# Denominators and first values of self-attention in one run of narrow products

## The chip, the core and the metric

The kernel runs on one core of one Trainium2 chip. A core has several engines that work at the same time, each with its own queue, which it works off in order: TensorE (PE in the profile, with its weight loads as PEld), VectorE (DVE), ScalarE (ACT), GpSimd (POOL), and SyncE (SP), which here mostly issues DMA transfers. They meet through semaphores. The metric is the device time of one execution in microseconds (us); less is better. The median of three runs stands for a kernel.

## The reference

A decoder layer (causal self-attention, cross-attention to 64 context rows, feed-forward), and then a gated fusion with the context. Only the self-attention matters here; batch 4, 1024 rows, 512 features, 16 heads of 32:

```python
B, T, TE, C, H = (2, 1024, 1024, 512, 16)   # the inputs have batch 4
DH = C // H
q = jnp.einsum('btc,hcd->bhtd', xn, Wq) + bq[None, :, None, :]
...
scale = DH ** (-0.5)
scores = jnp.einsum('bhtd,bhsd->bhts', q, k) / scale
...
scores = jnp.where(mask[None, None], scores, -jnp.inf)
attn = jax.nn.softmax(scores, axis=-1)
out = jnp.einsum('bhts,bhsd->bhtd', attn, v)
```

The kernel doesn't divide each weight by its row's sum. It sums `exp(score - max) * v` and, apart from that, `exp(score - max)` alone. The second is the denominator; cross-attention's first steps divide by it.

## The kernel before

Three phases follow each other: self-attention, cross-attention, feed-forward. Self-attention goes on until about 960 us of the profile, with cross-attention's first steps beginning shortly before that.

**Units.** Self-attention is cut into 32 units, one for each batch, group of four heads (4 x 32 = 128 partitions) and half of the eight row tiles: four tiles of 128 query rows, 512 columns (`TG`). For one pair of units per head group these are tiles (0, 1, 6, 7) and (2, 3, 4, 5); in the first pair (0..3) and (4..7). A unit goes over the blocks of 128 keys that its tiles can see: eight blocks or six. A later block is seen by fewer tiles, so it has fewer columns: 512, 384, 256 or 128. The blocks are taken in a written-out order, in the eight-block unit for instance 0, 7, 2, 1, 3, 6, 4, 5.

**One block.** `exps` makes transposed scores for each of the four heads (`st`, PE, line 677), their exponentials (ACT, line 682) into a pair of tiles `pT` with two heads each, and, where the block lies on the diagonal of one of the unit's tiles, zeroes what is masked (POOL, line 690). `weigh_all` makes the weighted values of two blocks at a time, one block after its exponentials: for each block four products with 32 columns of values as weights, one for each head (`av`, line 707), which add up in one bank over all blocks. Then `weigh` adds the block's `pT` pair to the pair of the unit's first block (POOL, now and then DVE, line 729), so that the first block's tiles end as the sum over all blocks. They are overwritten in place, so the first of these additions waits until the first block's own values are made.

**Denominators.** `sums` multiplies the finished pair with a matrix of ones, 128 x 32, again four products for the four heads (`den`, line 740), copies them out of PSUM (ACT, line 743) and stores them with one or two DMAs (SP, line 746). PSUM for `den` is one of the three banks that `st` uses. The values have one bank, copied out at the end of a unit (line 732).

The products `av` and `den` are fp32 with 128 x 32 weights: each is two records in the profile, and the four heads' products stand in four different groups of 32 columns. All other products of the phase have weights of 128 columns. They are called wide in this text, and `av` and `den` narrow.

**Beside it.** While a unit's blocks are worked, PE also makes the row maxima of later units (`s`, line 622, reduced by DVE) and projects queries, keys and values of later units (`pq`, `pk`, `pv`, line 116). `run` (line 129) merges such lists of steps by the share of each that is left. The resulting program is then reordered by a scheduler, which places each engine's instructions by priority and by its own idea of when they are ready. `tc.high_priority` raises the priority of what is written inside it; `tc.issue_after(x)` keeps instructions of x's engine behind x. In `weigh_all` the first product of a pair of blocks is written plainly, and the others are held behind it with a raised priority.

**Where the denominators are placed.** `attend` returns its steps and, apart from them, `sums` as a step of its own. The loop over the units puts the `sums` of one unit behind the first 12 steps of the next one's (`den_at` is 0, `HG` 4), and the last unit's after the loop.

Of the kernel before, what the change touches and what calls it, by code (L numbers as in the profile page):

```python
# [9 lines left out]
F32 = mybir.dt.float32  # L10
# [7 lines left out]
P = 128  # L18
B, T, C, H = 4, 1024, 512, 16
DH = C // H  # L20
# [4 lines left out]
TG = 512  # L25
NJ = TG // P
NG = T // TG
NT = T // P
HG = P // DH
# [22 lines left out]
def decoder_then_fusion(ctx: ExitStack, tc: tile.TileContext, x, ctxT, cols, rows,  # L52
                        Wq_s, Wk_s, Wv_s, W1, Wq_c, Wk_c, Wv_c, W2, Wf1, Wf2,
                        Wt, WvT, WgT, out):
    nc = tc.nc
# [73 lines left out]
    def run(*streams, speed=None, sooner=None):  # L129


        speed = [v for v, s in zip(speed or [1.0] * len(streams), streams) if s]
        sooner = [v for v, s in zip(sooner or [0] * len(streams), streams) if s]
        streams = [s for s in streams if s]
        left = [sum(t for t, _ in s) or 1 for s in streams]
        total, at = list(left), [0] * len(streams)
        while any(i < len(s) for i, s in zip(at, streams)):
            k = min((k for k in range(len(streams)) if at[k] < len(streams[k])),
                    key=lambda k: (1 - left[k] / total[k]) / speed[k])
            t, f = streams[k][at[k]]  # L140
# [65 lines left out]
    den_dram = dram_tiles("dend", groups, [H, TG])  # L206
# [180 lines left out]
    def self_attention(ph):  # L387
# [8 lines left out]
        outp = ph.enter_context(tc.tile_pool(name="out_a", reuse_waits="tile", bufs=2))  # L396
# [19 lines left out]
        def psum(name):  # L416
# [9 lines left out]
                                fill=MASKED, base=0, pattern=[[-1, P]], channel_multiplier=1)  # L426
# [4 lines left out]
        ones = cst.tile([P, DH], F32, tag="ones", name="ones")  # L431
# [14 lines left out]
        AHEAD = 4  # L446
# [120 lines left out]
        units = [(b, g, h, tiles) for b in range(B) for g in range(NC) for h, tiles in enumerate(tiles_of(b, g))]  # L567
        order = list(range(KST))
# [86 lines left out]
                nc.scalar.dma_start(raw(qs[KS + k : KS + k + 1].rearrange("p r (j q) -> p (r j) q", q=P)),  # L655
                                    raw(mT[k]))

        def attend(u):

            b, g, h, tiles = units[u]  # L660

            order = Z["o%d" % tiles[-1]] if tiles[0] != 4 else Z["o9"]
            first_col = [P * sum(tile < kb for tile in tiles) for kb in range(tiles[-1] + 1)]
            last = order[-1]
            held = {}
# [29 lines left out]
            def weigh_all(kbs):  # L695

                if kbs[0] == order[0]:
                    held["av"] = ps_av.tile([P, TG], F32, tag="av", name=f"av_{u}")
                    todo = [(kb, r) for kb in kbs for r in range(HG)[::-1]]
                else:  # L700
                    todo = [(kb, r) for kb in kbs[::-1] for r in range(HG)[::-1]]
                if kbs[-1] == last:
                    todo = [(kb, r) for kb in sorted(kbs, key=lambda k: k == last) for r in range(HG)[::-1]]

                def one(kb, r):
                    c0 = first_col[kb]
                    return nc.tensor.matmul(held["av"][r * DH : (r + 1) * DH, c0:],  # L707
                                            v_at[b, g][:, kb, r * DH : (r + 1) * DH],
                                            held[kb][r // 2][:, r % 2, c0:], start=kb == order[0], stop=kb == last)
                if Z["hp"]:  # L710
                    lead = todo[0]
                    first = one(*lead).ins
                    with tc.issue_after(first), tc.high_priority(offset=Z["hp"]):
                        for at in todo[1:]:
                            one(*at)
                else:
                    for at in todo:
                        one(*at)
                for kb in kbs:
                    weigh(kb)  # L720

# [13 lines left out]
                            nc.sync.dma_start(av_dram[b, n, g][:, shared[1]], avs[:, shared[0]])  # L735

            def sums():
                den = ps_of[Z["den"]][0].tile([P, TG], F32, tag=ps_of[Z["den"]][1], name=f"den_{u}")
                for r in range(HG)[::-1]:
                    nc.tensor.matmul(den[r * DH : (r + 1) * DH, :], ones, held[0][r // 2][:, r % 2, :],  # L740
                                     start=True, stop=True)
                dens = outp.tile([P, TG], F32, tag="dens", name=f"dens_{u}", bufs=1)
                nc.scalar.copy(dens, den)
                for n in range(NG):
                    if shared := columns(tiles, n):
                        nc.sync.dma_start(den_dram[b, n][g * HG : (g + 1) * HG, shared[1]], dens[::DH, shared[0]])

            groups_of = [order[i : i + Z["grp"]] for i in range(Z["grp0"], len(order), Z["grp"])]
            if Z["grp0"]:
# [3 lines left out]
            steps = []  # L753
            for i in range(len(order) + Z["lag"]):
# [75 lines left out]

        pieces[Z["pf"]].append((0, prefetch))
        begun = []
        before, first_late = [], len(units) - AHEAD
        for u in range(len(units)):
            if u and u + 2 < len(units):
                load_stacks(u + 2, u)
            main, after = attend(u)
            n = u % 2
            ahead, begun = begun, []
            if not ahead and u + 1 < len(units):  # L840
                ahead = maxima(u + 1)
            if u and u + 2 < len(units) and Z["phi%d" % n]:
                begun = maxima(u + 2)
                k = Z["phi%d" % n]
                first = begun[: k]
                first.insert(Z["tpl"], ahead.pop())
                ahead, begun = ahead + first, begun[k:]
            if u == first_late:
                fronts_of.close()
                rest = late_steps()  # L850
                total = sum(t for t, _ in rest)
            if u >= first_late:
                fill, part = [], Z["late"][u - first_late] * total
# [5 lines left out]
            run(main[: 3 * HG + Z["den_at"]] + before + main[3 * HG + Z["den_at"] :], ahead, fill, speed=(Z["main"], (Z["ahead%d" % n] if u < Z["alf"] else Z["ahead_l"]) if u else Z["a0"], Z["fill"]), sooner=(Z["so0"], Z["so1"], Z["so2"]))  # L859
            before = after  # L860
        run(before)
        switch(None)()


# [648 lines left out]
```

## Time and profile before

| What | us |
|---|---|
| Runs | 2229.69, 2229.91, 2230.17 |
| Median | 2229.91 |
| The profiled execution | 2232.46 |
| Its span, first to last instruction | 2230.7 |
| Granted clock of TensorE, mean | 0.976 |
| 256 records of `den`, first to last start | 118.8 to 955.2 |
| Copies of `den`, 32, median of one | 0.585 |
| Stores of `den`, 62, median of one issue on SP | 0.494 |
| 369 additions (line 729) on POOL, busy | 543.4 |
| 256 masks (line 690) on POOL, busy | 107.0 |

The page divides the span into 40 slices of 55.8 us. Each digit is a busy share in tenths:

```profile
PE   6899999999999998959999998999999999999997
...
POOL 3178778777977887865555423010115103410414
PEclk9899999999999999979999999999999999999998
```

The first seventeen slices are self-attention.

In the profile's timelines each row is a stretch of equal instructions: start, duration of the whole row, engine, line, operation, what is written and read, and xN for N records. A row's idle time and what ended it stand in square brackets, where there was any. Matmuls overlap: one begins before the last one has ended, so the distance between starts says more than the durations do. In the rows of waits the numbers are the sum in us, the count, and the longest.

### The profile page before, as it was taken

The page shows a single profiled execution, that of the slowest core. Times are in us where ns is not written, and L with a number is a line of the kernel's source. Part 1 is how long each engine was busy: PE and PEld are TensorE (multiplying, and loading weights), DVE is VectorE, ACT ScalarE, POOL GpSimd, SP SyncE. Part 2 cuts the span into 40 slices and gives each one's busy share as a digit, 9 for nine tenths or more (in the row PEclk, how much of TensorE's full clock was granted, in tenths as well). Part 3 has the DMA queues.
Part 4 walks back from the last instruction along what each step waited for, and adds up shares of the span by engine and source line. Part 5 has one row for each costly group of instructions (what it writes and reads, how often), then busy time and mean ns, then how long its engine had stood idle before and what let it go on. Part 6 is the DMA issues. An engine that isn't in the chain of part 4 may idle for free.

```text
span 2230.7 us, 34011 instructions
## 1 busy us (share of the span) xinstructions
PE 2121.8 (95%) x11724; PEld 1607.5 (72%) x11724; DVE 1293.2 (58%) x2829; ACT 982.3 (44%) x2171; POOL 1091.8 (49%) x1156
## 2 busy tenths in 40 slices
PE   6899999999999998959999998999999999999997
PEld 5666676667666655548788886888887887888785
DVE  6476657665656678687878765341337225531727
ACT  3355455545555555435555565432233324322432
POOL 3178778777977887865555423010115103410414
PEclk9899999999999999979999999999999999999998
DMA  8855666655656475432222214644345425342531
GB/s 247 239 166 163 179 175 179 171 172 169 190 149 188 127 210 177 155 97 67 86 76 76 91 48 156 195 164 142 127 140 206 166 98 207 138 175 85 207 133 47
DMA packets 204386, 333.68 MB, mean 150 GB/s; under 512 B 28460, under 2 KB 91676, under 8 KB 202934
## 3 DMA queue, kind: packets, MB, share of 16 engines
q1 hardware_dynamic: 186364, 314.68, 45.1%
q10 hardware_dynamic: 17850, 16.83, 2.5%
q8 instruction: 93, 1.52, 0.3%
q14 instruction: 79, 0.65, 0.1%
HBM read 231.78 MB, written 99.12 MB: 148 GB/s over the span
## 4 chain that ended last, share of the span: by engine, by line
PE 77%; DVE 9%; DMA 5%; issue 5%; ACT 2%; POOL 1%; SPq 1%; DVEq 0%; POOLq 0%; ACTq 0%
PE ph_f L116 13%; PE acc_f L1251 13%; PE st L677 6%; PE s L622 6%; PE av L707 5%; PE pk L116 4%; PE po_c L116 4%; PE pv L116 4%; PE pq L116 4%; PE pq_x L116 3%; PE po_x L116 3%; PE pg_o L116 3%; PE sc_c L104 2%; PE av_c L1030 2%; PE tpp_c L1017 1%
## 5 line engine op out<-in xcount | busy, mean ns | idle before, releaser
L729 POOL TENSOR_TENSOR pT<-pT,pT 128x512 f32<-128x512 f32 (+3 forms) x369 | 543.4, 1495 | 34.8 <-PE av L707 29.3
L1251 PE MATMUL acc_f<-wf,hs_f 128*128 128x512 f32 x1536 | 385.6, 394 | 9.1 <-DVE hs_f L74 5.9
L116 PE MATMUL ph_f<-xn_f,wf 128*128 128x512 f32 x1536 | 382.5, 394 | 4.0 <-DVE xn_f L74 3.3
L682 ACT ACTIVATE pT<-st 128x512 f32<-128x512 f32 (+2 forms) x640 | 319.9, 560 | 128.4 <-PE st L677 87.4
L1251 PEld LDWEIGHTS acc_f<-wf,hs_f 128*128 128x128 f32 x1536 | 285.2, 188 | 72.6 <-DVE hs_f L74 8.1
L116 PEld LDWEIGHTS ph_f<-xn_f,wf 128*128 128x128 f32 x1536 | 288.5, 189 | 66.0 <-DVE xn_f L74 3.7
L627 DVE CUSTOM_DVE_ANT_0 s<-s,mask 128x512 f32<-128x512 f32 (+3 forms) x512 | 245.4, 503 | 142.1 <-PE s L622 140.9
L622 PE MATMUL s<-ks,qs 96*128 96x512 f32 (+3 forms) x768 | 253.4, 373 | 23.8 <-DMA qs<-qd 6.5
L1230 ACT ACTIVATE ph_f<-ph_f,colv 128x512 f32<-128x512 f32 x128 | 84.4, 659 | 393.5 <-PE ph_f L116 385.3
L74 DVE TENSOR_TENSOR hs_f<-ph_f,hs_f 128x512 fp32r<-128x512 f32 x128 | 87.8, 686 | 284.1 <-ACT hs_f L73 284.0
L630 DVE TENSOR_REDUCE top<-s 128x1 f32<-128x512 f32 x256 | 175.7, 686 | 100.8 <-PE s L622 100.2
L677 PE MATMUL st<-qs,ks 98*128 98x256 f32 (+2 forms) x888 | 230.8, 340 | 2.6 <-DMA qs<-mT 1.3
L622 PEld LDWEIGHTS s<-ks,qs 96*128 96x128 f32 x768 | 140.6, 194 | 108.9 <-DVE top L630 23.3
L677 PEld LDWEIGHTS st<-qs,ks 98*128 98x128 f32 x888 | 151.8, 192 | 68.1 <-ACT pT L682 37.1
L1226 POOL TENSOR_TENSOR y_f<-y_f,row_bf 128x512 f32<-128x512 f32 x32 | 42.0, 1317 | 314.1 <-DMA y_f<-x 231.4
L690 POOL TENSOR_SCALAR_AFFINE_SELECT pT<-pT 128x256 f32<-128x256 f32 x256 | 107.0, 434 | 163.6 <-ACT pT L682 126.8
L707 PE MATMUL av<-pT,v 128*32 128x512 f32 (+3 forms) x1776 | 159.1, 456 | 1.6 <-ACT pT L682 1.0
L1366 POOL TENSOR_TENSOR g_o<-g_o,z_o 128x512 f32<-128x512 f32 x28 | 41.8, 1504 | 176.4 <-DVE g_o L1365 173.5
L1009 POOL TENSOR_TENSOR p_c<-p_c,inv_c 128x512 f32<-128x512 f32 x64 | 69.0, 1078 | 107.1 <-DVE inv_c L1008 85.5
L116 PE MATMUL pv<-wv,xn_s 128*128 128x256 f32 x768 | 113.7, 298 | 4.2 <-ACT vout L527 3.0
L116 PEld LDWEIGHTS pv<-wv,xn_s 128*128 128x128 f32 x768 | 106.0, 202 | 14.4 <-issue 3.7
L116 PE MATMUL pk<-xn_s,wk 128*128 128x512 f32 x384 | 107.4, 422 | 6.4 <-DVE xn_s L74 3.0
(226 smaller groups left out, 3554.9 us busy)
## 6 DMA issues: line engine op xcount, KB each, us to landing
wf<-wf2d SPq DMA_DIRECT2D x84, 512.0 KB
ks<-kd SPq DMA_DIRECT2D x96, 256.0 KB
qs<-qd SPq DMA_DIRECT2D x96, 256.0 KB
kd<-k SPq DMA_DIRECT2D x64, 256.0 KB
qd<-q SPq DMA_DIRECT2D x120, 128.0 KB
wf<-wf1d SPq DMA_DIRECT2D x28, 512.0 KB
x<-in_x SPq DMA_DIRECT2D x32, 256.0 KB
wk<-wk SPq DMA_DIRECT2D x16, 512.0 KB
```

Of the source, the lines that this page charges most:

```text
L74: (lo_eng or nc.vector).tensor_tensor(lo, src, hi, ALU.subtract)
L116: nc.tensor.matmul(held["ps"], a_at(a()[i], c), b_at(b()[j], c), start=c == 0 and k == 0, stop=c == NC - 1 and k == 2)
L622: nc.tensor.matmul(sc[:, :w], q_at[u][:KS, r, j * P : (j + 1) * P], k_at[u, m][:KS, r, :w], start=True, stop=True)
L627: nc.vector.tensor_tensor_reduce(sc[:, :w], sc[:, :w], mask[:, TG - w :], 1.0, TOP, ALU.add, ALU.min, dst)
L630: nc.vector.tensor_reduce(dst, sc, AX.X, ALU.min)
L677: nc.tensor.matmul(st[:, i], k_at[u, kb // NJ][:KM, r + i, (kb % NJ) * P : (kb % NJ + 1) * P], q_at[u][:KM, r + i, c0:], start=True, stop= ...
L682: nc.scalar.activation(held[kb][(r + i) // 2][:, at : at + k, c0:], st[:, i : i + k], AF.Exp, scale=-QSCALE)
L690: nc.gpsimd.affine_select(out=t, in_=t, compare_op=ALU.is_ge, fill=0.0, base=0, pattern=[[0, 2], [1, P]], channel_multiplier=-1)
L707: return nc.tensor.matmul(held["av"][r * DH : (r + 1) * DH, c0:], v_at[b, g][:, kb, r * DH : (r + 1) * DH], held[kb][r // 2][:, r % 2, c0: ...
L729: eng.tensor_tensor(t[:, :, c0:], t[:, :, c0:], p[:, :, c0:], ALU.add)
L1230: nc.scalar.activation(ps, ps, AF.Relu, bias=col("bf1", f))
L1251: mm = nc.tensor.matmul(acc[j], held[f][i0][:, j * P : (j + 1) * P], w[2, f][:, i1], start=f == 0 and m == 0, stop=last and m == 2)
```

## The change

`sums` no longer runs as a step. It hands out its first product, the other three, and what is to be done at the end (copy and stores). `attend` of the next unit gets these as `tail`, and in the first `weigh_all` of that unit, that of its first two blocks, the first product of the denominators is written plainly; the other three and the eight products of values are held behind it with the raised priority; then come the copy and the stores of the denominators. The step of the denominators between the first twelve and the other steps is gone, and the branch for a raised priority of 0 as well. After the last unit its denominators are made as before. The number of products, additions, copies and stores is the same.

```diff
-        def attend(u):
+        def attend(u, tail):
...
-                if Z["hp"]:
-                    lead = todo[0]
-                    first = one(*lead).ins
-                    with tc.issue_after(first), tc.high_priority(offset=Z["hp"]):
-                        for at in todo[1:]:
-                            one(*at)
+                if kbs[0] == order[0] and tail:
+                    lead, others, end = tail()
+                    others += [lambda at=at: one(*at) for at in todo]
                 else:
-                    for at in todo:
-                        one(*at)
+                    lead, *others = [lambda at=at: one(*at) for at in todo]
+                    end = lambda: None
+                first = lead().ins
+                with tc.issue_after(first), tc.high_priority(offset=Z["hp"]):
+                    for product in others:
+                        product()
+                end()
                 for kb in kbs:
                     weigh(kb)
...
             def sums():
+
                 den = ps_of[Z["den"]][0].tile([P, TG], F32, tag=ps_of[Z["den"]][1], name=f"den_{u}")
-                for r in range(HG)[::-1]:
-                    nc.tensor.matmul(den[r * DH : (r + 1) * DH, :], ones, held[0][r // 2][:, r % 2, :],
-                                     start=True, stop=True)
-                dens = outp.tile([P, TG], F32, tag="dens", name=f"dens_{u}", bufs=1)
-                nc.scalar.copy(dens, den)
-                for n in range(NG):
-                    if shared := columns(tiles, n):
-                        nc.sync.dma_start(den_dram[b, n][g * HG : (g + 1) * HG, shared[1]], dens[::DH, shared[0]])
+
+                def product(r):
+                    return nc.tensor.matmul(den[r * DH : (r + 1) * DH, :], ones, held[0][r // 2][:, r % 2, :],
+                                            start=True, stop=True)
+
+                def end():
+                    dens = outp.tile([P, TG], F32, tag="dens", name=f"dens_{u}", bufs=1)
+                    nc.scalar.copy(dens, den)
+                    for n in range(NG):
+                        if shared := columns(tiles, n):
+                            nc.sync.dma_start(den_dram[b, n][g * HG : (g + 1) * HG, shared[1]],
+                                              dens[::DH, shared[0]])
+
+                first, *others = [lambda r=r: product(r) for r in range(HG)[::-1]]
+                return first, others, end
...
-            return steps, [(5 * TG, sums)]
+            return steps, sums
...
-        before, first_late = [], len(units) - AHEAD
+        tail, first_late = None, len(units) - AHEAD
         for u in range(len(units)):
...
-            main, after = attend(u)
+            main, tail = attend(u, tail)
...
-            run(main[: 3 * HG + Z["den_at"]] + before + main[3 * HG + Z["den_at"] :], ahead, fill, ...)
-            before = after
-        run(before)
+            run(main, ahead, fill, ...)
+        first, others, end = tail()
+        first()
+        for product in others:
+            product()
+        end()
```

More of the change, by code (lines that the diff above doesn't have):

```diff
@@ L858, in self_attention @@
                 fill = pieces[u + AHEAD]
-            run(main[: 3 * HG + Z["den_at"]] + before + main[3 * HG + Z["den_at"] :], ahead, fill, speed=(Z["main"], (Z["ahead%d" % n] if u < Z["alf"] else Z["ahead_l"]) if u else Z["a0"], Z["fill"]), sooner=(Z["so0"], Z["so1"], Z["so2"]))
-            before = after
-        run(before)
+            run(main, ahead, fill, speed=(Z["main"], (Z["ahead%d" % n] if u < Z["alf"] else Z["ahead_l"]) if u else Z["a0"], Z["fill"]), sooner=(Z["so0"], Z["so1"], Z["so2"]))
+        first, others, end = tail()
[3 more added lines that the diff above has]
+        end()
         switch(None)()
```

## The prediction

> **What bounds the kernel now.** I read the page's busy shares first, then busy time by stretch of 100 us, then what PE and POOL wait for, then PE's timeline. The change touches self-attention alone, so the stretches that count lie before 960 us.
>
> ```profile
> PE 2121.8 (95%) x11724; PEld 1607.5 (72%) x11724; DVE 1293.2 (58%) x2829; ACT 982.3 (44%) x2171; POOL 1091.8 (49%) x1156
> ...
> core 0: us, PE busy (x) PEld busy (x) DVE busy (x) ACT busy (x) POOL busy (x), PEclk, DMA share, GB/s
> ...
> 300.00:400.00 100.00, 97.10 (x644) 66.00 (x643) 63.31 (x189) 54.94 (x110) 80.95 (x86) 0.98 0.60 176
> ...
> 700.00:800.00 100.00, 99.41 (x678) 68.97 (x677) 64.07 (x198) 52.90 (x106) 81.82 (x82) 1.00 0.58 158
> ```
>
> PE is idle for 2.9 and 0.6 us of these 100 (3.4 is the most in any stretch from 200 to 800), at an almost full granted clock. POOL is next with 81. DMA has 0.6. So self-attention is PE's to shorten, as long as POOL keeps pace.
>
> ```profile
> 334.18 1.06 PE L707 MATMUL av<-pT,v 128*32 128x512 f32 x8
> 335.18 0.50 PE L677 MATMUL st<-qs,ks 98*128 98x512 f32 x1
> 335.52 0.34 PE L622 MATMUL s<-ks,qs 96*128 96x384 f32 x1
> ...
> 336.74 0.43 PE L707 MATMUL av<-pT,v 128*32 128x128 f32 x8
> 337.09 0.33 PE L622 MATMUL s<-ks,qs 96*128 96x128 f32 x1
> ...
> 337.90 0.39 PE L622 MATMUL s<-ks,qs 96*128 96x512 f32 x1
> 338.22 1.06 PE L740 MATMUL den<-pT,ones 128*32 128x512 f32 x8
> 339.22 0.67 PE L622 MATMUL s<-ks,qs 96*128 96x384 f32 x2
> ...
> 339.97 0.40 PE L622 MATMUL s<-ks,qs 96*128 96x512 f32 x1
> 340.20 0.40 PE L677 MATMUL st<-qs,ks 98*128 98x512 f32 x1
> ```
>
> This is PE's timeline at the start of unit 9: its first block of values (av, 512 columns), its second (av, 128 columns), the denominators of unit 8 (den), each a run of its own between wide products. Four products are eight records: each fp32 product is two, and the four column groups work at once. Read the starts, since durations overlap. From 338.22 to 339.22 the den run takes 1.00; the 128-column run takes 337.09 - 336.74 = 0.35. The 0.65 between them pays for 2 x 384 more columns, 0.846 ns a column, so two rounds of 512 stream for 0.87 and 0.13 of the run is fixed. Entering costs too: a 512-wide product is followed after 0.23 (339.97 to 340.20), but den starts 0.32 after the one at 337.90: 0.09. Leaving too: the st product at 335.18 is followed after 0.34 instead of 0.24: 0.10. Sum 0.32. Done to the nanosecond over all 192 such runs, the median is 0.34 us (0.335 for den alone), and it is the same for 8, 16 and 24 records: a price per run, not per product.
>
> With it PE's time can be added up. From 100 to 800 us there are 160 runs: 54 us of this price, 125 us of narrow streaming, 478 us of wide products at their usual spacing, and 42 us of anything else.
>
> **The change, part by part.** The order in which the two built programs issue is known, though not timed.
>
> *Runs removed.* Narrow runs go from 192 to 154. Den, first and second block stood in three runs for nearly every unit. In the changed order they are one run of 12 products in 14 of the 31 unit boundaries, a run of 8 and one of 4 in 13, and four runs in 4 (before units 10, 18, 26, 30), where the scheduler cuts den into two halves. 38 x 0.335 = 12.7 us less PE time, with nothing beside it that could hide it.
>
> *Den cut in halves.* A half uses two of the four column groups for the same 2 x 0.43, so each cut costs 0.86 us of streaming: 4 x 0.86 = 3.4, less the one such cut before (one product, then three): +2.6 us.
>
> A rule of the skill speaks against the main term. "TensorE: Matmul & The Clock Gate", Part 3 (Measured speedup vs the span model), gives a packed group the duration of one product plus some 4 ns for each further tile. That has no price for entering or leaving, and by it 38 fewer runs save nothing and the sum below would end at +6 us. In the trace the products of a round do start 7 ns apart, but the 0.34 us around them stand in every run, whatever its length, so the row decides.
>
> *Values later, POOL later.* Den now leads, and the first block's values follow it. Measured against the neighbouring wide products, den stands 1 to 5 us earlier than before, the first values 0.4 to 1.7 us later in most units, 2 to 4 us in six and 10 in the last.
>
> ```profile
> POOL pT L690 <- ACT pT L682: 108.0, 41, 6.6
> ...
> POOL pT L729 <- PE av L707: 26.2, 29, 2.0
> ...
> PE den L740 <- DVE mv_x L183: 4.1, 1, 4.1
> ...
> PE av L707 <- ACT pT L682: 1.0, 2, 0.5
> ```
>
> What is late next is POOL's first addition (L729): it overwrites the first block's weights and so waits for their values, already 26.2 us in 29 places. Behind it on POOL stand the masks (L690) of later blocks, and PE's values of those blocks wait for them. Before the change the tightest masked block of a unit is ready 0.6 us or less ahead of its product in 24 of units 1 to 30. There is little cover, so each microsecond of POOL's delay could reach PE. Against it, POOL's new order puts the middle masks one addition (1.2 to 2.4 us) earlier in most units. Laying POOL's new order, with its measured durations, against the new starts of the products leaves about 1 us short in units 8, 16, 22 and 24 and about level elsewhere. I take +3 us. Bounds: no wait at all, even 3 us fewer of those present (12.7 us stand inside or next to runs from 100 to 800 us), and 12 us if every shortfall is paid in full.
>
> Den itself waits for the unit's last addition. That was over 5.7 to 12.4 us ahead of it in units 1 to 30; less den's advance and POOL's delay, 1 us or more remains everywhere. Nothing is taken for it; it is in the bound of 12. What would be held is the whole run of 12 and all of PE behind it, since PE issues in order.
>
> *Copy and stores.* The copy of den (32 of 0.585 us on ACT) moves one block of exponentials ahead, and its two stores ahead of about one key-stack load on SP. ACT is busy 55 of 100 us and waits 87 us for st products, and SP's loads are two units ahead of use; that is the cover. Without it a copy late by 0.6 us in each unit would delay exponentials by 19 us in all, which PE sees only once the three st banks are full. 0.
>
> *The end.* The last den waits for POOL and DVE in the trace, with PE idle for 4.1 us before 955.15 and 0.6 before the values. The last unit's first values come 10 us later among PE's work, but more of cross-attention's opening is issued ahead of them. From the second block's values to the last den PE has 20.9 us of work in the new order, 22.6 before, where 29.3 passed; POOL's chain from the first addition, in the trace's durations, is about 26 (24 of its own and DVE's last addition, 2.6). So the idle time stays at 5 to 8 us against 6.7. I take +0.5, bounds -3 and +3.
>
> Sum: -12.7 + 2.6 + 3 + 0 + 0.5 = **-6.6 us**. The profiled execution took 2232.46 us, 2230.7 of it span; the span becomes 2224. The median of the runs shown is 2229.91, 2.5 below the profiled one, so 2223.
>
> **The rivals.** About 0.2%, 4.5 us, is what a measurement of this kernel can tell from no change.
>
> *The full gain.* Waits don't grow: -12.7 + 2.6 = -10, and if some waits inside the joined runs and at the end vanish too, up to -16: 2214 to 2220. For it: den is ready long before, and one joined run has one place to wait instead of three. Against it: first values come later everywhere.
>
> *A wash.* The waits take 6 to 12 us in place of 3, which gives -3.6 to +2.4, with the end at +3 up to +5: 2226 to 2235. For it: the 0.6 us cover and POOL's 81 of 100. Against it: POOL's idle 19 in 100 gives some back, and the masks were moved forward.
>
> *Slower.* One mechanism: the joined run delays POOL's first addition, POOL becomes the bound of every unit, and PE stops each time at a masked block's values. At 0.7 us in each of 31 units that is 21.7 - 10.1 = +12, 2242. It decides from (10.1 + 4.5) / 31 = 0.47 us a unit. For it: the same tight blocks recur in every batch. Against it: the additions are the same in number, and PE's waits for POOL or ACT are about 1 us in the stretches above.
>
> *Not doing what it says.* Excluded in the main: the order shows 8 runs of den alone against 33. It is the 2.6 us term.
>
> **How the numbers follow.** The forecast and its own range, 2220 to 2225, have 0.44; the full gain 0.17; the wash 0.23; slower 0.16. Faster by over 0.2% is 0.61, within 0.23, slower 0.16. Range: -16 at the bottom (2214), and at the top the waits' bound 12 in place of 3 with the end at +3 gives +5; the slower case is left with little beyond 2232, so 2213 to 2232.
>
> **What would show it.** Right: in PE's timeline at unit boundaries one row of den x8 followed directly by av x16, or av x8 and a short run; first addition's wait for av rising from 26 towards 40 us; PE's wait rows for POOL masks staying under some 5 us; den's idle time only at the end. Wrong: the price per run is not saved when runs join (a joined run longer than its rounds plus 0.13), or PE rows "av <- POOL" of 10 us and more, or a longer idle stretch before the last den.

## The result and the profile after

The changed kernel is a little slower: median 2234.85 us of 20 runs (2230.78 to 2245.08) against 2230.23 (2225.55 to 2237.00) for the kernel before, ratio 1.0026, 95% interval 1.0016 to 1.0036. The forecast of 2223 and its range, 2213 to 2232, both missed. The profiled execution took 2234.50, its span is 2232.8 against 2230.7.

The view of busy time by stretch tells at once where to look. First the kernel before (columns as in the prediction: PE, PEld, DVE, ACT, POOL busy with their records, PE's granted clock, DMA share, GB/s), then the changed one.

```profile
100.00:800.00 700.00, 684.77 (x4513) 472.26 (x4512) 452.79 (x1320) 375.04 (x748) 550.20 (x566) 0.99 0.60 170
800.00:960.00 160.00, 141.56 (x784) 83.41 (x783) 123.88 (x227) 77.46 (x151) 130.06 (x119) 0.91 0.60 181
```

```profile
100.00:800.00 700.00, 682.51 (x4555) 474.06 (x4554) 450.92 (x1334) 379.11 (x760) 558.11 (x572) 1.00 0.62 172
800.00:960.00 160.00, 131.83 (x729) 80.91 (x733) 118.13 (x212) 69.76 (x135) 126.53 (x118) 0.90 0.59 175
```

From 100 to 800 us PE gets through 42 records more in slightly less busy time: the kernel is ahead. From 800 to 960 us it is busy for 131.8 of 160 us where it was busy for 141.6. What self-attention's body gains, its last few units lose.

The joined run itself looks as forecast. PE's timeline of the changed kernel at the start of unit 9:

```profile
328.89 1.07 PE L745 MATMUL den<-pT,ones 128*32 128x512 f32 x8
329.77 1.26 PE L708 MATMUL av<-pT,v 128*32 128x512 f32 x16
330.96 0.33 PE L622 MATMUL s<-ks,qs 96*128 96x128 f32 x1
```

Denominators of unit 8, first and second values of unit 9 stand in one run of 330.96 - 328.89 = 2.07 us. Two rounds of 512, two of 512 and two of 128 columns are 0.43 x 4 + 0.107 x 2 = 1.93, so 0.14 is fixed: one price, where three runs paid three.

To see where the time goes, each record's distance to the next start was set against the usual distance for its kind in the kernel before, and the surplus sorted: at a narrow run, at half clock, a wait (over 0.35 us), a smaller gap. From the first scores of unit 1 to those of unit 27, in us:

| | before | changed |
|---|---|---|
| Length | 680.7 | 671.9 |
| Usual distances | 585.8 | 585.8 |
| Price of runs (157, 126 of them) | 53.2 | 45.1 |
| Denominators cut in halves (1, 3) | 0.8 | 2.5 |
| Waits | 17.5 | 18.2 |
| Smaller gaps | 15.2 | 18.7 |
| Half clock | 8.2 | 1.6 |

The rest was cut at starts that the timelines show: the first scores of units 27, 30 and 31, the last denominators, and the end (the start of PE's last product, some 15 us ahead of the span's end). The same cuts were made in every experiment; the table of them stands behind the experiments. Here it is 86.7 against 86.6 for units 27 to 29, 36.5 against 43.8 for unit 30, 42.0 against 49.1 for unit 31, and 1260.1 against 1258.0 from there on. So 8.8 us are gained in the body, and 14.4 lost in the last two units. With 2.1 gained behind them and 1.5 ahead of unit 1 that is the +2 of the span.

Unit 31 in PE's timeline, before and then after: its first scores, its first values, its last block of values, and (after) the denominators.

```profile
913.18 0.96 PE L677 MATMUL st<-qs,ks 98*128 98x512 f32 x3
...
918.61 1.07 PE L707 MATMUL av<-pT,v 128*32 128x512 f32 x8
...
949.73 0.85 PE L707 MATMUL av<-pT,v 128*32 128x384 f32 x8 [0.60 <-POOL pT L690]
```

```profile
910.21 0.97 PE L678 MATMUL st<-qs,ks 98*128 98x512 f32 x3
...
925.37 1.26 PE L708 MATMUL av<-pT,v 128*32 128x512 f32 x16
...
948.06 1.11 PE L961 MATMUL tpn_x<-ident,xh_x 128*128 128x128 f32 x4 [3.63 <-DVE x_x L948]
...
958.05 1.51 PE L708 MATMUL av<-pT,v 128*32 128x384 f32 x8 [5.97 <-POOL pT L691]
959.34 1.73 PE L745 MATMUL den<-pT,ones 128*32 128x512 f32 x8
```

The unit begins 3 us earlier than before, its first values come 7 us later, since they now follow unit 30's denominators, and its last block waits 6 us for a mask on POOL. POOL's timeline of the changed kernel shows why the mask is late:

```profile
941.11 2.72 POOL L928 TENSOR_TENSOR sav_x<-sav_x,inv_x 128x512 f32<-128x512 f32 x2
...
944.51 2.35 POOL L732 TENSOR_TENSOR pT<-pT,pT 128x1024 f32<-128x1024 f32 x1
...
948.91 1.27 POOL L928 TENSOR_TENSOR sav_x<-sav_x,inv_x 128x512 f32<-128x512 f32 x1
950.15 2.35 POOL L732 TENSOR_TENSOR pT<-pT,pT 128x1024 f32<-128x1024 f32 x1
...
953.84 2.13 POOL L732 TENSOR_TENSOR pT<-pT,pT 128x768 f32<-128x768 f32 x1
955.93 1.71 POOL L928 TENSOR_TENSOR sav_x<-sav_x,inv_x 128x512 f32<-128x512 f32 x1
957.60 0.40 POOL L691 TENSOR_SCALAR_AFFINE_SELECT pT<-pT 128x256 f32<-128x256 f32 x1
```

The last mask (957.60) stands behind the additions of the unit (L732) and behind multiplications of cross-attention's third and fourth groups (sav_x, L928). Its exponentials had been done since 945.7. In the kernel before, both masks of this block were through at 949.7, ahead of the last addition:

```profile
948.57 1.10 POOL L690 TENSOR_SCALAR_AFFINE_SELECT pT<-pT 128x256 f32<-128x256 f32 x2
...
952.30 1.89 POOL L729 TENSOR_TENSOR pT<-pT,pT 128x768 f32<-128x768 f32 x1
```

### The profile page after: what moved, and what is told of

Read it like the earlier page. It is cut to its first block, busy times and chain, and to the rows that moved or that the text cites. A ratio compares the mean times of both kernels' runs of the same rounds, so it can differ in the third digit from the quotient of the medians.

```text
span 2232.8 us, 33991 instructions
## 1 busy us (share of the span) xinstructions
PE 2110.1 (95%) x11724; PEld 1606.4 (72%) x11724; DVE 1283.5 (57%) x2829; ACT 981.7 (44%) x2171; POOL 1092.3 (49%) x1156
## 4 chain that ended last, share of the span: by engine, by line
PE 70%; DVE 9%; DMA 7%; issue 5%; POOL 5%; ACT 3%; SPq 1%; DVEq 0%; ACTq 0%; POOLq 0%
PE ph_f L116 13%; PE acc_f L1265 13%; PE s L622 5%; PE av L708 5%; PE st L678 4%; PE pq_x L116 4%; PE po_c L116 4%; POOL pT L732 3%; PE po_x L116 3%; PE pk L116 3%; PE pg_o L116 3%; PE pv L116 3%; PE pq L116 2%; PE sc_c L104 2%; PE av_c L1044 1%
## 5 line engine op out<-in xcount | busy, mean ns | idle before, releaser
L732 POOL TENSOR_TENSOR pT<-pT,pT 128x256 f32<-128x256 f32 (+3 forms) x369 | 545.9, 1500 | 86.5 <-PE av L708 77.9
L622 PE MATMUL s<-ks,qs 96*128 96x512 f32 (+3 forms) x768 | 248.6, 372 | 25.0 <-DVE least L627 8.4
L116 PE MATMUL pv<-wv,xn_s 128*128 128x256 f32 x768 | 108.3, 291 | 4.9 <-ACT vout L527 2.3
```

What stands on the lines that cost most here:

```text
L116: nc.tensor.matmul(held["ps"], a_at(a()[i], c), b_at(b()[j], c), start=c == 0 and k == 0, stop=c == NC - 1 and k == 2)
L622: nc.tensor.matmul(sc[:, :w], q_at[u][:KS, r, j * P : (j + 1) * P], k_at[u, m][:KS, r, :w], start=True, stop=True)
L732: eng.tensor_tensor(t[:, :, c0:], t[:, :, c0:], p[:, :, c0:], ALU.add)
```

## The experiments

All are built from one file, in which a set of units says where the change is made; with all units in it PE's instructions are those of the changed kernel, with none those of the kernel before.

```diff
+JOIN = set(range(32))
...
-            main, tail = attend(u, tail)
+            old, joined = tail, u in JOIN
+            main, tail = attend(u, old if joined else None)
+            if old and not joined:
+                main.insert(3 * HG, (5 * TG, lambda old=old: apart(old)))
```

`apart` makes the four denominators and their end as a step of its own. `range(n)` ends at n - 1, and unit 0 has nothing to join. The kernels of one group ran on one chip, each group on another, with the kernel before beside them; ratios are to that. The same kernel came out up to 0.23% apart on two chips (`e11` and `e15` below), so small steps are read within a group. Medians are of 12 runs where nothing else is said.

**Group 1: body or end?** The theories: (A) joining gains some 10 us in the body, and the order that the scheduler gives to the end as a consequence, above all VectorE's in cross-attention's opening, costs more; (B) the end of self-attention is a floor, and a faster body can't show. What speaks for A is PE's longest wait around 980 us, for the last split of the first group's normalised rows, 9.5 us before. After the change:

```profile
PE pq_x L116 <- DVE xn_x L74: 18.9, 1, 18.9
```

On VectorE that split stands behind four splits of W2 and three copies of block-diagonal keys before, behind four splits and twelve copies and differences after.

`e1_join_to25`: `JOIN = set(range(26))`.

> The change for units 1 to 25 alone; from unit 26 on the denominators are a step of their own, as before. 157 narrow runs instead of 192 (before) and 154 (the whole change). Theory A (the joined runs save their 10 us in the body, and the new order that the end got costs more than that): the body is 10 to 12 us ahead of before at unit 25 and most of it stays, 2219 to 2224. Theory B (the end is a floor, set by other engines, and waits away whatever PE gains ahead of it): ahead at unit 25, and within 3 us of before at the end, 2228 to 2233.

Measured: 2223.92, ratio 0.9953 (0.9938 to 0.9969).

`e2_join_from28`: `JOIN = {28, 29, 30, 31}`.

> The change for units 28 to 31 alone; up to unit 27 all is as before. 187 narrow runs. In its order on DVE the last split of the first normalised tile stands behind twelve copies and differences of the spread keys and four splits of W2, as in the whole change. Theory A: nothing is gained ahead, and the end alone is slower by what the whole change lost there, +8 to +14 us, 2238 to 2244. Theory B: the end is the same floor, within 3 us of before.

Measured: 2238.41, ratio 1.0021 (1.0003 to 1.0038), with 6.4 us of wait at the last block's mask and 17.3 at the split.

`e3_all_fix` and `e4_none_fix`: the whole change, and the kernel before, with a hold. `turned_all` is the last split of the first group; W2's splits, the loads of the third group, and the copies of the keys may not go ahead of it on VectorE:

```diff
             def spread_keys():
+                with tc.issue_after(turned_all):
+                    spread_keys_now()
...
             run(ends[1][1][k:], ends[0][2])
+            turned_all = latest["lo"]
...
-            with gate:
+            with gate, tc.issue_after(turned_all):
                 load_w2()
                 run(ends[2][0])
```

> The whole change, and in cross-attention's opening the spread keys' copies, the splits of W2 and the group loaded after them are held on DVE behind the last split of the first normalised tile. If that order is what the end pays for (A, in the opening): the 18.9 us wait of the query products falls under 8, and the time to 2222 to 2228. If the loss stands before it, in units 28 to 31, or the opening is bound by the work itself (B): 2231 to 2236, with the wait in another place.

Measured: 2225.08, ratio 0.9967 (0.9951 to 0.9983).

> The kernel before with the same hold on DVE alone, to tell the hold's own worth from the change's. Before, the split stood behind three copies and four splits of W2, and the query products waited 9.5 and 4.2 us. A: a gain of 2 to 5 us, less than in the whole change. B: within 2 us of before.

Measured: 2229.24, ratio 0.9985 (0.9968 to 1.0002). So the body's gain is real and shows in the time when the end is left alone (e1); B falls. The last four units alone cost as much as the whole change (e2). The hold is worth 0.59% in the changed kernel, read across two chips (0.31% by the later pair `e13` and `e18`, on two chips as well), and 0.15% in the one before, where the interval reaches no change. That fits A, but the hold moves more than one thing.

**Group 2: which part of the end?**

`e5_no_cuts_hold`: `JOIN = set(range(32)) - {10, 18, 26, 30}` with the hold. (6 runs.)

> The change in all units except 10, 18, 26 and 30, whose denominators of the unit before stay a run of their own (148 narrow runs in the built order, none of them a den cut in halves), with cross-attention's opening held in the order of the earlier held kernels. Theory A: 44 runs fewer at 0.335 us are -14.7, the one cut den of the kernel before gone -0.9, waits +3, the hold -3: about -12 to -16 us, ratio 0.993 to 0.995, some 4 us below the whole change with the hold. Theory B (a floor at the end): no lower than 0.9967.

Measured: 2223.16, ratio 0.9951 (0.9933 to 0.9970).

`e6_none_behind`: no joins; VectorE's order forced.

```diff
-                split(xn[0][:, c, :], xn[1][:, c, :], tp, f"{uid}_{c}")
+                hold = ExitStack()
+                if (b, n) == groups[0] and c == NC - 1:
+                    hold = tc.issue_after(spread(kbd[b % 2], b))
+                with hold:
+                    split(xn[0][:, c, :], xn[1][:, c, :], tp, f"{uid}_{c}")
```

> The kernel before, no runs joined (192 runs as before); only the order of VectorE in cross-attention's opening is forced to that of the changed kernel: the last split of the first group's normalised rows is held behind all twelve copies and differences of the first block-diagonal keys (before the change three copies stood ahead of it). Theory A (this order costs the end of the changed kernel its gain): PE's wait of pq_x for xn_x rises from 9.5 to 17 us or more, and the kernel is 4 to 9 us slower, ratio 1.002 to 1.004. Theory B (the order there is harmless, the end is bound by something else): ratio within 0.999 to 1.001.

Measured: 2233.12, ratio 1.0001 (0.9987 to 1.0015). `spread` makes all the copies and differences of the first group's keys. The wait grew, though less than A expected:

```profile
PE pq_x L118 <- DVE xn_x L76: 21.3, 2, 12.3
```

The two waits of this row make 21.3 us against 13.7 before (9.5 and 4.2), and the kernel is no slower. So this order costs little by itself: PE waits longer for the split, but the keys have to be made anyway, and later waits of 2.5 us for queries and 1.0 for keys are gone. From the last denominators to the end it is 1261.3 us against 1260.1. The longest wait, 12.3 us, fell short of the changed kernel's 18.9, so this alone doesn't exclude A; the next run does.

`e7_hold_keys`: the whole change, of the hold only the part in `spread_keys`.

> The whole change (154 runs), with only the copies and differences of the block-diagonal keys held behind the last split on VectorE; the four splits of W2 stay ahead of it. If the keys were what stood in the way: most of the hold's gain is there, ratio 0.997 to 0.999, pq_x waits for xn_x 6 to 11 us. If the splits of W2 were (they wait for their own loads and ScalarE): ratio stays at 1.002 or more and pq_x waits 15 us or more.

Measured: 2235.79, ratio 1.0012 (0.9998 to 1.0026). The wait for the split fell to 1.9 us, and nearly nothing was gained; unit 31 takes 49.0 us as in the changed kernel. The changed kernel itself stands at 1.0010 and 1.0026 on two other chips. So the keys' place isn't what costs, nor is PE's wait for the split, and A falls.

`e8_join_to29`: `JOIN = set(range(29))`, nothing held. The set ends at 28: units 29, 30 and 31 are as before, one more than the name and the expectation say. PE's timeline bears it out: the denominators made in unit 29 stand in a run of their own, at 857.6 us.

> The change in units 1 to 29, the last two units as before (157 runs), nothing held; in the order that results only the four splits of W2 stand between the third and the last split of the first group's rows on VectorE. Theory A: the body's gain of about 10 us is kept, ratio 0.994 to 0.998. Theory B, the gain is lost as soon as the units near the end are joined: 1.000 to 1.003.

Measured: 2224.91, ratio 0.9956 (0.9942 to 0.9971). Twenty-eight of the 31 boundaries may be joined with the full gain; the loss belongs to the last three.

**Group 3: GpSimd's chain.** With e6 and e7 a new theory was needed. (C): in the last unit the joined run starts the additions later, and GpSimd's chain of additions, masks and cross-attention's multiplications then sets the end. The hold works because the third group's multiplications follow their loads out of that chain.

`e9_hold_mult`: the whole change, and only this:

```diff
-                nc.gpsimd.tensor_tensor(av, av, inv, ALU.mult)
+                with ExitStack() if (b, n) in groups[:2] else tc.issue_after(latest["mask"]):
+                    nc.gpsimd.tensor_tensor(av, av, inv, ALU.mult)
```

`latest["mask"]` is the last mask of self-attention.

> The whole change (154 runs, joins in the last units too). One thing is held: on GpSimd, the multiplications of weighted values by inverse denominators for cross-attention's third and later groups (1.3 us each) stand behind the last mask of self-attention, where six of them stand among the last unit's additions and masks in the changed kernel. Theory C (the joined run starts the last unit's additions later, and GpSimd's chain of additions, masks and these multiplications then sets the end of self-attention): the six, 8 us of GpSimd time, leave that chain, and the kernel is 8 to 13 us faster than the changed one, ratio to before 0.996 to 0.999. Theory A (the order on VectorE): in this build the last split stands ahead of W2 and the keys by itself, so it expects the same; the run of the last unit alone and the forced order of e6 tell the two apart. Theory B (a floor at the end): 1.000 or more.

Measured: 2231.10, ratio 1.0006 (0.9991 to 1.0020). POOL's timeline in the last unit:

```profile
945.35 2.40 POOL L734 TENSOR_TENSOR pT<-pT,pT 128x1024 f32<-128x1024 f32 x1
...
949.03 2.39 POOL L734 TENSOR_TENSOR pT<-pT,pT 128x1024 f32<-128x1024 f32 x1
...
952.13 2.27 POOL L734 TENSOR_TENSOR pT<-pT,pT 128x768 f32<-128x768 f32 x1
...
955.71 0.41 POOL L693 TENSOR_SCALAR_AFFINE_SELECT pT<-pT 128x256 f32<-128x256 f32 x1
956.08 3.23 POOL L937 TENSOR_TENSOR sav_x<-sav_x,inv_x 128x512 f32<-128x512 f32 x2
```

The additions now follow each other by 3.1 to 3.7 us instead of 3.7 to 5.6, and the multiplications come behind the mask. PE's wait at the last block shrinks from 5.97 to 1.99 us, and unit 31 from 49.1 to 39.7. That part of C is shown: these multiplications in the chain are a large part of what makes unit 31 long. The whole kernel gains less than expected, since unit 30 is as long as before (44.1), and the stretch from the last denominators on is 1259.7, longer than in the changed kernel: part of what was moved may be paid there.

`e10_join_last`: `JOIN = {31}`.

> Only the last unit's boundary is joined (190 runs), nothing held. On VectorE nothing but normalisations stands between the first group's splits, which is better than in the kernel before; on GpSimd four multiplications of the third group stand among the last unit's additions. Theory A (VectorE's order): not slower, ratio 0.997 to 1.0005. Theory C (GpSimd's chain starts later in the last unit): PE waits 3 us or more at the last masked block, the stretch from the last unit's first scores to its denominators grows by 4 us or more, and the kernel is 2 to 7 us slower, ratio 1.001 to 1.003.

Measured: 2232.84, ratio 1.0013 (0.9998 to 1.0027). Unit 31 takes 46.1 us where it took 42.0: the 4 us of C in the profile, though the wait stands at the transposes (4.8 us for VectorE's sum of x), not at the mask as expected. By the ratio the loss is some 3 us, and its interval just reaches no change.

`e11_join_to30`: `JOIN = set(range(31))`.

> The change in all units but the last (156 runs), nothing held; four splits of W2 stand ahead of the last split on VectorE. Theory C: GpSimd's chain of the last unit starts as before, the body's gain stays, ratio 0.995 to 0.998. Theory A, by the four splits: 0.998 to 1.001. If joining unit 30 costs by itself (units 27 to 31 took some 8 us more than their work in the changed kernel), 0.999 to 1.001.

Measured: 2235.05, ratio 1.0016 (1.0003 to 1.0029). This misses C's range: something ahead of unit 31's boundary costs as well. Against e8 two boundaries were added, those of units 29 and 30.

`e12_to25_no_cuts_hold`: `JOIN = set(range(26)) - {10, 18}`, with the wide hold.

> A version meant to beat both: joined in units 1 to 25 except 10 and 18, where den would be cut in halves (154 runs, no cut), the last six units as before, and cross-attention's loads, W2 splits and keys held as in the earlier held kernels, which keeps the multiplications out of the last unit's chain. By the price per run -12.7 -0.9, waits +3, and the hold's -3: about -12 to -15 us, ratio 0.993 to 0.9955. With a floor at the end: 0.996 or more.

Measured: 2226.76, ratio 0.9976 (0.9960 to 0.9993). Faster, but less than either part promised, and less than e1, which has two cuts and no hold (0.9953, on another chip).

**Group 4: unit 30 or the chip?** The contrast between e8 (joined to 28) and e11 (to 30) stood on two chips.

`e13_change`: the change. `e14_join_to29`: the same kernel as e8, so joined to 28. `e15_join_to30`: the same as e11. `e16_to29_no_cuts_hold`: `JOIN = set(range(30)) - {10, 18, 26}` with the hold (10 runs; e14 has 11); this one does join unit 29.

> The change itself again, on one chip with the three that follow, since the runs so far stand on different chips. All theories: ratio 1.001 to 1.004. In the stretch from unit 27 to the first cross scores some 10 to 13 us more is lost than in the kernel before, of it about 7 between the last unit's first values and its denominators (theory C, GpSimd's chain); the body before it is 6 to 9 us shorter.

Measured: 2233.78, ratio 1.0010 (1.0000 to 1.0021).

> The same kernel as in the run that joined units 1 to 29: ratio 0.994 to 0.997 if what was seen there holds on this chip; 0.998 or more would say that the earlier difference to the run with unit 30 lay in the chip.

Measured: 2223.35, ratio 0.9962 (0.9948 to 0.9977).

> Unit 30 joined as well. If joining unit 30 itself costs (its den is cut in halves, its first values come later, and the last unit's first scores come behind it): 3 us or more above the kernel joined to 29, ratio 0.998 to 1.002. Theory C alone (the last unit's boundary): within 2 us of it.

Measured: 2228.98, ratio 0.9993 (0.9980 to 1.0006).

> Joined in units 1 to 29 except 10, 18 and 26 (151 runs, none cut), the last two units as before, with the hold of the earlier held kernels, which keeps the third group's multiplications out of the last unit's chain on GpSimd. Theory C: the best of the four, 2 to 6 us below the kernel joined to 29, ratio 0.992 to 0.996. With a floor at the end: equal to it.

Measured: 2222.20, ratio 0.9970 (0.9955 to 0.9984). On one chip the steps stand apart: joining units 29 and 30 takes 0.31% (some 6 us), joining unit 31 another 0.17% (4.8 us by the medians, though the two intervals still overlap). Units 29 and 30 weren't added one at a time. Where unit 31 isn't joined, the hold shortens it too: from 42.8 us in e17, below, which differs in the hold alone, to 38.2. From the last denominators to the end some 2 us of it are given back.

**Group 5: the hold again, and the cuts.** `e17_to29_no_cuts`: as e16 without the hold. `e18_all_hold`: the same kernel as e3.

> Joined in units 1 to 29 except 10, 18 and 26, nothing held (151 runs; one den cut in halves, as in the kernel before, against three in the kernel joined to 29). By the price of a cut, 0.86 us, and of a run: 1.7 plus 6 runs at 0.3, some 3 us below the kernel joined to 29, ratio 0.993 to 0.996. If the cut dens were not what the ledger makes of them: equal to it or above, 0.996 to 0.998.

Measured: 2228.26, ratio 0.9983 (0.9969 to 0.9997). Without cuts in its joined boundaries it is no faster than e8 and e14, rather slower. But it joins unit 29, which they don't, so the three boundaries left out aren't the only difference, and what a cut costs in time isn't settled by this pair.

> The whole change with the wide hold (W2, the third group's loads and multiplications, and the keys) once more, on another chip than before. Theory C with the loss at the last two units: the last unit's stretch is again some 12 us shorter than in the changed kernel, ratio 0.996 to 0.998. If the earlier gain lay in the chip: 0.999 or more.

Measured: 2226.59, ratio 0.9979 (0.9967 to 0.9992). The hold's gain on the whole change stands on a second chip.

The lengths of the stretches, one profiled execution each, in us:

| | Units 1-26 | 27-29 | 30 | 31 | last den to end | ratio |
|---|---|---|---|---|---|---|
| before | 680.7 | 86.7 | 36.5 | 42.0 | 1260.1 | 1 |
| changed | 671.9 | 86.6 | 43.8 | 49.1 | 1258.0 | 1.0026 |
| e13, changed | 671.8 | 86.0 | 43.9 | 48.4 | 1255.1 | 1.0010 |
| e2, 28 to 31 | 684.5 | 82.2 | 44.6 | 48.3 | 1254.8 | 1.0021 |
| e7, all, keys held | 676.4 | 90.8 | 44.8 | 49.0 | 1254.6 | 1.0012 |
| e10, 31 alone | 686.0 | 90.0 | 36.0 | 46.1 | 1258.5 | 1.0013 |
| e15, to 30 | 670.7 | 87.0 | 44.1 | 45.1 | 1255.2 | 0.9993 |
| e11, to 30 | 675.8 | 88.3 | 43.8 | 45.9 | 1253.4 | 1.0016 |
| e14, to 28 | 673.7 | 86.0 | 38.0 | 45.1 | 1252.0 | 0.9962 |
| e8, to 28 | 674.5 | 86.8 | 37.4 | 45.6 | 1254.3 | 0.9956 |
| e1, to 25 | 674.0 | 91.0 | 36.9 | 42.2 | 1257.2 | 0.9953 |
| e9, all, multiplications held | 680.0 | 87.5 | 44.1 | 39.7 | 1259.7 | 1.0006 |
| e3, all, wide hold | 678.2 | 86.5 | 43.8 | 39.0 | 1254.5 | 0.9967 |
| e18, all, wide hold | 678.7 | 89.5 | 46.1 | 38.7 | 1250.7 | 0.9979 |
| e16, to 29, no cuts, wide hold | 674.0 | 87.1 | 40.5 | 38.2 | 1258.0 | 0.9970 |
| e17, to 29, no cuts | 680.7 | 84.1 | 40.5 | 42.8 | 1255.9 | 0.9983 |
| e5, to 31 but 30, no cuts, wide hold | 679.3 | 89.0 | 40.5 | 38.1 | 1258.2 | 0.9951 |
| e12, to 25, no cuts, wide hold | 674.8 | 91.4 | 36.0 | 36.7 | 1252.6 | 0.9976 |
| e4, none, wide hold | 681.6 | 89.6 | 35.6 | 37.2 | 1257.3 | 0.9985 |
| e6, none, order forced | 684.4 | 89.8 | 35.4 | 42.0 | 1261.3 | 1.0001 |

The first column varies by several us from one execution to the next; units 30 and 31 vary less, and there a pattern shows. Unit 30 takes 43.8 us or more where it is joined, 40.5 where unit 29 is joined and 30 isn't (e5, e16, e17), and 35.4 to 38.0 where neither is. So, by single profiles that agree, some 3 us of its loss come with unit 29's boundary and some 3.5 with its own.

Unit 31 goes with how many multiplications of the third and fourth groups stand in GpSimd's order ahead of its last addition or mask. With none it takes 36.7 to 39.7 us (the held kernels), with four or five 42.0 to 46.1, with six 48.3 to 49.1 (the changed kernel, e13, e2 and e7). Joining adds to it: with none some 1.5 us (36.7 to 38.2 unjoined in e4, e12 and e16, 38.1 to 39.7 joined in e3, e5, e9 and e18), with four 4.1 us (e10 against the kernel before). But e8, e14, e11 and e15 don't join unit 31, have five, and take 45.1 to 45.9.

The versions that beat both kernels by most are those joined to 25 (0.9953) and to 28 (0.9956 and 0.9962) with nothing else, and e5 (0.9951, 6 runs); their intervals overlap. The first is the simplest.

## Why the prediction was wrong

**Runs removed, -12.7.** Right in kind, a fifth too large. The body has 31 runs fewer, forecast at 0.335 each 10.4 us, and the price of runs fell by 53.2 - 45.1 = 8.1. A run still pays 0.14 inside and 0.10 on leaving, but entering costs 0.12 on average instead of 0.10.

**Den cut in halves, +2.6.** 2.5 - 0.8 in the body and 0.8 for the fourth cut, in unit 30: 2.5 in all. No two kernels differ in the cuts alone, so its worth in time isn't shown.

**Values later, POOL later, +3.** PE's waits in the body are 0.7 us more, the smaller gaps 3.5. From 200 to 800 us PE waits 3.4 us for POOL's masks in 11 places, each at most 0.6. In size that part came as forecast. What came otherwise (the first row up to 960 us, the second from 200 to 800 us):

```profile
POOL pT L732 <- PE av L708: 74.8, 27, 5.7
```

```profile
PE st L678 <- DMA qs<-mT: 4.6, 7, 1.1
```

POOL's additions wait 74.8 us for values up to 960 us, not some 40, and PE's waits for masks in the body stayed at those 3.4. And scores wait 4.6 us from 200 to 800 us for the DMA that brings the row maxima into the query stack (`qs<-mT`), where 0.4 stood before. ScalarE issues this DMA, not SP, and the prediction had no term for it. What makes it late wasn't tried.

**The rivals.** POOL as the bound of every unit is excluded by units 1 to 26. But its mechanism, the joined run delaying the first addition until a masked block's values stop PE, is what happens in the last unit, with cross-attention's multiplications added to POOL's chain.

**The end, +0.5, bounds -3 and +3.** This is the step that failed: units 30 and 31 lost 14.4 us, 2.1 of it given back behind them, so the term measured +12.3. The sign that the prediction named for this is there: PE stands for 3.63 and 5.97 us in the last unit, against 0.6 and 4.09 before. Its forecast of 5 to 8 us of idle time there became 9.8. Three things were wrong.

First, the step saw that the last unit's first values come behind more work, and took POOL's chain from the first addition, about 26 us, as given. In the new order six multiplications of the third and fourth groups, 1.3 to 1.7 us each, stand in that chain or just ahead of it, against four of the third before, and the last mask has moved behind the last addition. From the second block's values to the last denominators it was 33.1 us (926.2 to 959.3), against 29.3 before. e9 shows it by taking these multiplications out: 9.4 us less in unit 31. For the whole kernel e9 shows less, 1.0006 against 1.0010 and 1.0026 on other chips.

Second, a stall is mostly paid twice, as the last section shows.

Third, it looked at the last unit only. Unit 30 lost 7.3 us. Its waits of 0.25 us and more make 7.5 us against 4.0, among them 5.0 for the split of cross-attention's value weights on VectorE; before, PE's wait for such a split (2.1 us, key weights) fell into unit 29. The cut denominators are 0.8; the rest, half clock and other work, wasn't told apart. e14 and e15, which differ in the boundaries of units 29 and 30, confirm the place but not the reason, since both wait for that split:

```profile
871.40 3.91 PE L118 MATMUL pvc<-wvc,ct 128*128 128x512 f32 x9 [3.78 <-DVE wvc L76]
```

```profile
876.13 3.78 PE L118 MATMUL pvc<-wvc,ct 128*128 128x512 f32 x8 [4.94 <-DVE wvc L76]
```

So the wait for the split is 1.2 us longer where the two units are joined, and unit 30 is 6.1 us longer. What makes it so stays open.

The sum by stretches is -8.8 for the body and +14.4 - 2.1 for what follows, +3.5; the medians differ by 4.6, and on the other chip by 2.4. The body was forecast at -5.7 (31 runs, two cuts more and the waits: -10.4 + 1.7 + 3), so the whole miss lies in the end. That the body did better than that is luck as far as the forecast goes: runs, cuts, waits and smaller gaps make -8.1 + 1.7 + 0.7 + 3.5 = -2.2, and 6.6 us came from half clock that fell away, which the forecast didn't have.

**The range.** Its top doesn't follow from the sum: +5 us on 2229.9 is 2235, and the wash reaches 2235 as well, but the range stops at 2232.

## What to carry to other kernels

A saving per occurrence holds where the pattern repeats, and the boundary cases have to be costed one by one: here 28 of 31 boundaries gave the gain and the last three took it back and more, so make such a change with a switch for each place, and look in the trace whether the switch did what it was set to. Where a scheduler decides, read the new order of every engine around the end of a phase and add up the slowest engine's chain in it, foreign work included. A long wait in a profile isn't yet a cost: ask what would have been waited for next, and change the suspected order alone before believing it.

## What was not expected of the hardware

**A stall of 2 us is mostly followed by half clock.** In the kernel before PE waits 1.94 us for a row maximum at 245.41, and 1.75 at 453.83. The stretches around them, before and then after the change, where these waits are gone (the number ahead of the DMA share is the granted clock):

```profile
240.00:255.00 15.00, 13.05 (x80) 9.92 (x79) 8.31 (x21) 3.35 (x8) 11.60 (x11) 0.89 0.62 159
450.00:465.00 15.00, 12.70 (x70) 9.50 (x69) 7.97 (x18) 2.84 (x7) 10.19 (x8) 0.77 0.58 137
```

```profile
240.00:255.00 15.00, 14.92 (x107) 11.20 (x106) 8.03 (x25) 6.81 (x15) 10.59 (x10) 1.00 0.73 212
450.00:465.00 15.00, 14.76 (x99) 10.88 (x102) 9.18 (x32) 8.62 (x19) 10.06 (x13) 1.00 0.52 161
```

0.89 of 15 us is 3.4 us at half clock, 0.77 is 6.8. In the body this is a gain of 6.6 us, larger than what the new waits took; in the changed kernel's last unit it is a loss: after the stall of 3.63 us at 948.06 eight records of values, 1.06 us elsewhere, take 1.94. In the 20 profiles of this case, between 120 and 800 us, PE waited 1.7 to 2.3 us 33 times, and in 31 of them half clock set in during the wait or within 2 us behind it; of 56 waits of 1.0 to 1.6 us it was 7. It isn't certain even for the same wait: in e4 the one of 1.94 us at 455.50 was followed by full clock (1.00 from 450 to 465 us). The Trainium skill, "TensorE: Matmul & The Clock Gate", section "HAM oscillation", gives as an abstract rule that idle gaps over some 3.4 us are to be avoided; here gaps of 1.75 and 1.94 us were followed by half clock too.

**Runs differ.** The kernel before took 2222.9 to 2242 us over all groups, and single profiles of kernels that share a body differ by 9 us in it. Differences below some 5 us were told by medians of a dozen runs, or by stretches that repeat, never by one span.
